# A state-space convolution, two adapter layers and a gated FFN on one core: group 3's tables earlier, later chunks' results through DRAM, 29 weights ahead

## The chip, the core and the metric

The kernel runs on one core of one Trainium2 chip. The metric is the device time of one execution, in microseconds. All data is float32. The engines named below are TensorE (PE, matmuls), VectorE (DVE), ScalarE (ACT), GpSimd (POOL) and SyncE (SP), which only issues transfers. All transfers of the core run on the same 16 DMA engines.

## The reference

Four residual layers on x of shape (32, 64, 1024), that is batch B, channels H, positions L:

```python
x = x + ssm(x, log_dt, C, log_A_real, A_imag, D, length)     # y*mask, y = irfft(rfft(u)*rfft(K)) + u*D
x = x + einsum('bsi,boi->bso', x, w1[adapter_ids])           # 1024 x 1024 of 16, one per batch row
x = x + einsum('bij,bkj->bik', x, w2[adapter_ids2])
x = x + down(silu(gate(x)) * up(x))                          # 1024 -> 2752 -> 1024, each with a rank-16 LoRA
```

K is the convolution filter of a channel, `2*Re(sum_n Ct[n]*exp(dtA[n]*l))` for l below 1024. The first layer is thus a causal convolution along the 1024 positions, separately for 64 channels; `mask` cuts it off at each row's length. The second and third need one 4 MB matrix for each batch row and layer, the fourth the same three matrices for all rows.

## The kernel before

Rows are worked in four chunks of eight batch rows (512 columns); a chunk is a tile `x` of 128 positions x 8 x 512. TensorE executes in program order; on the other engines a scheduler places the instructions, with `issue_after` as a lower bound where it is written.

**Setup and convolution** (`convolution`, from line 600). SyncE loads the parameters (`par`), constants, lengths and then x of all four chunks (L624; chunks 2 and 3 lie in a pool on the right side of SBUF). VectorE, ScalarE and GpSimd make the filters of the 64 channels in nine groups of 4, 4, 8, ... 8 channels (`kernels(g)`): GpSimd multiplies out `rho` and `br` (L698), VectorE reduces angles (L645), ScalarE takes exponentials and sines, VectorE forms `et` and `gt` (the last at L791). TensorE then multiplies `gt` and `et` into a PSUM tile `pk` (L804), after a matmul (L795) that puts the D of each channel into it: its moving operand `dk` is a mostly zero tile of 32 columns a channel, filled by GpSimd. ScalarE copies `pk` to `ks` and stores it to DRAM as `kp`, one tensor a group, each with 128 zeros ahead (L815, L816).

`convolve` takes four channels at a time: it loads the reversed x of these channels (`uf`), then for each pair of channels the filter's shifted rows from DRAM (`hk`, L833, three buffers), does 32 matmuls (L845), and VectorE applies the mask (`tmp`). At the end GpSimd adds `tmp` to the x of each of the four chunks (L861). Groups 0 and 1 are made ahead; group g+2 is made after the first four channels of group g. So TensorE's stream reads: tables 0 and 1, channels 0 to 3, table 2, channels 4 to 7, table 3, channels 8 to 11, table 4, and so on.

**Adapters** (`adapter`, L163). One adapter is eight weight tiles of 512 KB (`wa`, rows taken by the batch row's index, L179) and 64 matmuls (L184). VectorE transposes the result and adds it to x (L195, L197). The 16 adapters of chunk 0 run by themselves. Their first nine weights go to tiles `early`, loaded where SyncE has room after the sixth filter load; all later weights of the kernel, those of the FFN too, share a pool `wpool` of nine tiles of 512 KB. A weight's tile is given again once its last reader is done.

**FFN** (`ffn`, L458). `rest` (L401) multiplies the odd columns left over. `gated` (L346) then runs ten times, with two steps each (gate, up). A step loads two weight tiles (`wf`), VectorE forms sums of them (`stationary`), and TensorE does seven products of four matmuls (L361) where eight would be plain (Strassen-like); VectorE collects them in `c` (L378 to L390). After each step `between` is called: at step 0 of chunk 0 it parks x of chunks 2 and 3 in DRAM and gives their place to the activations' pool `apool`; at step 0 of chunks 1 and 2 it loads the next x from there; and at each step it runs `other(4)`, which spreads the 16 adapters of the next chunk over the 20 steps (4 shares each) and five of the eight down-projection parts (5 shares each): 16 adapters in 105 shares. The down projection (L558) follows in two blocks, with the outputs of the chunk stored at the end.

Of the kernel before, what the change touches and what calls it, by code (L numbers as in the profile page):

```python
# [8 lines left out]
F32 = mybir.dt.float32  # L9
I32 = mybir.dt.int32  # L10
AF = mybir.ActivationFunctionType
ALU = mybir.AluOpType
# [4 lines left out]
P = 128  # L17
B, H, L = 32, 64, 1024
NS = 64
KT = L // P  # L20
# [9 lines left out]
EARLY = 9  # L30
# [6 lines left out]
NPIECE = 2 * BC  # L37
AT_GATED, AT_DOWN = 4, 5
# [27 lines left out]
def kernel(  # L66
# [44 lines left out]
    def x_tile(pool, c, tag):  # L111
        return pool.tile([P, KT, TC], F32, tag=tag, name=f"x{c}")

    ctx.enter_context(tc.manual_schedule(engines={PE}))
    xs = [x_tile(xpool, c, "x") for c in range(2)]

    right = ExitStack()
    x2pool = right.enter_context(tc.tile_pool(name="x2pool", bufs=1, side="right"))
    first = right.enter_context(ExitStack())
    epool = first.enter_context(tc.tile_pool(name="epool", bufs=1, side="right"))  # L120
    late = [x_tile(x2pool, c, f"x{c}") for c in range(2, NCK)]
    early = [epool.tile([P, L], F32, tag=f"e{i}", name=f"early{i}") for i in range(EARLY)]
    blocks = convolution(tc, cst, consts, xt, xf, ssm, lens, xs + late, ps_tile)
    parked = []

    def park():
        for c, x_c in enumerate(late, 2):
            d = dpool.tile([P, KT, TC], F32, tag=f"xd{c}", name=f"xd{c}")
            nc.gpsimd.dma_start(d, x_c)
            parked.append(d)  # L130

    ids_sb = cpool.tile([1, 3 * B], I32, tag="ids", name="ids_sb")
    nc.sync.dma_start(ids_sb, ids)

# [25 lines left out]
    loads = []  # L160
    ypool = ctx.enter_context(tc.tile_pool(name="ypool", bufs=2, reuse_waits="tile"))

    def adapter(w, layer, b):  # L163
        c, lo = b // BC, (b % BC) * H
        with ExitStack() as after:
            if len(loads) > 3:

                after.enter_context(tc.issue_after(loads[-4]))
            e = nc.values_load(
                ids_sb[0:1, layer * B + b : layer * B + b + 1],  # L170
                engines=[SP],
                min_val=0,
                max_val=NE - 1,
            )
        acc = ps_tile(f"pa{layer}_{b}")
        for kt in range(KT):
            name = f"wa{layer}_{b}_{kt}"
            wt = early.pop(0) if early else wpool.tile([P, L], F32, tag="w", name=name)
            load = nc.sync.dma_start(  # L179
                wt, w[bass.ds(e, 1), kt].rearrange("e p f -> p (e f)")  # L180
            )
# [11 lines left out]
        loads.append(load.ins)  # L193
# [5 lines left out]
    def adapters(c):  # L199


        for b in range(c * BC, (c + 1) * BC + 1):
            if b < (c + 1) * BC:
                yield adapter(w1, 0, b)
            if b > c * BC:
                yield adapter(w2, 1, b - 1)

    with tc.issue_after(blocks[5]):

        pieces = adapters(0)  # L210
        for _ in range(3):
            next(pieces)
    for _ in pieces:
        pass
# [18 lines left out]
    apools = []  # L233
# [112 lines left out]
    def gated(c, m, xb, between):  # L346
# [4 lines left out]
        for g, w in enumerate((wg, wu)):  # L351
# [38 lines left out]
            nc.vector.tensor_add(cf, cf, lt[:, g].rearrange("p i t -> p (i t)"))  # L390
# [3 lines left out]
        act = apools[0].tile([P, 2, TC], F32, tag="act", name=f"act_{c}_{m}")  # L394
# [63 lines left out]
    def ffn(c, xb, others):  # L458
# [6 lines left out]
        def other(share, of=2 * FM * AT_GATED + (2 * KH - 3) * AT_DOWN):  # L465
            due[0] += share * NPIECE
            while due[1] * of < due[0]:
                next(others, None)
                due[1] += 1

        def between(i):
            if i == 0 and c == 0:
                with tc.issue_after(cols[-1]):
                    park()
                right.close()
                apools.append(
                    ctx.enter_context(
                        tc.tile_pool(
                            name="apool", bufs=MB, side="right", reuse_waits="tile"
                        )  # L480
                    )
                )
            if i == 0 and c and c + 1 < NCK:
                x_n = x_tile(xpool, c + 1, "x")
                nc.sync.dma_start(x_n, parked[c - 1])
                xs.append(x_n)
            other(AT_GATED)
# [3 lines left out]
        for block, (m0, m1) in enumerate(BLOCKS):  # L491
# [7 lines left out]
            if last:  # L499
# [3 lines left out]
                for t in (0, 1):  # L503
                    wl_t = wl[:, t].rearrange("p i f -> p (i f)")
                    gather(wl_t[FIRST], bd, rows_half[FIRST, c, t : t + 1])
                    nc.sync.dma_start(wl_t[SECOND], wd_rest)
# [5 lines left out]
            for i, act in enumerate(acts):  # L512
                t3 = apools[0].tile([P, 4, TH], F32, tag="actd", name=f"actd_{c}_{m0 + i}")
# [86 lines left out]
def convolution(tc, cst, consts, xt, xf, ssm, lens, xs, ps_tile):  # L600
# [9 lines left out]
    with ExitStack() as ctx:  # L610
# [12 lines left out]
        for c in range(NCK):  # L623
            nc.sync.dma_start(xs[c], xt[:, c])  # L624
# [141 lines left out]
        zero = s1.tile([HG, P], F32, tag="zero", name="zero")  # L766
        nc.vector.memset(zero, 0.0)


        dk = s1.tile([P, HG, LQ], F32, tag="dk", name="dk")  # L770
        nc.gpsimd.memset(dk, 0.0)

        def kernels(g):
# [3 lines left out]
            r = powers(g, y, s1, "r")  # L777
            nc.gpsimd.tensor_copy(dk[0:1, :n, 0], dskip[0:1, h0 : h0 + n])
# [15 lines left out]
            ps = ps_tile(f"pk{g}")[:LQ, : n * LQ]  # L794
            nc.tensor.matmul(  # L795
                ps,
                cst[:, CO_SEL : CO_SEL + LQ],
                dk[:, :n].rearrange("p h l -> p (h l)"),
                start=True,
                stop=False,  # L800
                skip_group_check=True,
            )
            for i in range(n):
                nc.tensor.matmul(  # L804
                    ps[:, i * LQ : (i + 1) * LQ],
                    gt[:, i, :],
                    et[:, i, :],
# [227 lines left out]
```

## Time and profile before

| | us |
|---|---|
| median of three runs (2400.56 to 2403.77) | 2400.56 |
| the profiled execution, whole | 2400.47 |
| its span, first to last instruction | 2398.8 |
| TensorE busy | 2324.7 (97%) |
| VectorE busy | 1087.4 (45%) |
| ScalarE busy | 310.8 (13%) |
| GpSimd busy | 206.8 (9%) |

A profile shows one execution. The span is cut into 40 slices of about 60 us; a digit is the busy share of an engine in tenths, and GB/s is what the DMA engines moved:

```profile
PE   4998888999999999999999999999999999999999
DVE  7511113454344543554344533554444544554653
DMA  7889997656656646656756646655756543223311
GB/s 274 286 290 369 408 408 273 217 211 210 228 202 226 226 149 213 228 202 211 244 189 244 208 148 215 242 189 201 269 182 248 185 158 115 82 84 108 99 55 62
```

The first slice is the setup, up to the third or fourth is the convolution, the next three are chunk 0's adapters, and all the rest are the four FFNs. A group of the profile names line, engine, operation, `out<-in` by tile names (buffer numbers left out), and what the engine waited for before it.

### The profile page before, as it was taken

The page shows a single profiled execution, that of the slowest core. Times are in us where ns is not written, and L with a number is a line of the kernel's source. Part 1 is how long each engine was busy: PE and PEld are TensorE (multiplying, and loading weights), DVE is VectorE, ACT ScalarE, POOL GpSimd, SP SyncE. Part 2 cuts the span into 40 slices and gives each one's busy share as a digit, 9 for nine tenths or more (in the row PEclk, how much of TensorE's full clock was granted, in tenths as well). Part 3 has the DMA queues.
Part 4 walks back from the last instruction along what each step waited for, and adds up shares of the span by engine and source line. Part 5 has one row for each costly group of instructions (what it writes and reads, how often), then busy time and mean ns, then how long its engine had stood idle before and what let it go on. Part 6 is the DMA issues. An engine that isn't in the chain of part 4 may idle for free.

```text
span 2398.8 us, 46172 instructions
## 1 busy us (share of the span) xinstructions
PE 2324.7 (97%) x19154; PEld 1837.2 (77%) x19154; DVE 1087.4 (45%) x2067; ACT 310.8 (13%) x605; POOL 206.8 (9%) x301
## 2 busy tenths in 40 slices
PE   4998888999999999999999999999999999999999
PEld 3995335787787786788787786788787787888888
DVE  7511113454344543554344533554444544554653
ACT  4200002110011101110011101110011101210210
POOL 3533001000000020000000020000000020000000
PEclk9999999999999999999999999999999999999999
DMA  7889997656656646656756646655756543223311
GB/s 274 286 290 369 408 408 273 217 211 210 228 202 226 226 149 213 228 202 211 244 189 244 208 148 215 242 189 201 269 182 248 185 158 115 82 84 108 99 55 62
DMA packets 163139, 501.21 MB, mean 209 GB/s; under 512 B 20018, under 2 KB 54130, under 8 KB 161906
## 3 DMA queue, kind: packets, MB, share of 16 engines
q1 hardware_dynamic: 146434, 461.78, 55.2%
q0 software_dynamic: 9568, 27.80, 3.6%
q10 hardware_dynamic: 6928, 8.69, 1.0%
q8 instruction: 151, 2.47, 0.4%
q14 instruction: 58, 0.48, 0.1%
HBM read 485.31 MB, written 12.88 MB: 208 GB/s over the span
## 4 chain that ended last, share of the span: by engine, by line
PE 90%; DMA 7%; DVE 1%; ACT 1%; issue 0%; POOL 0%; SPq 0%; ACTq 0%; DVEq 0%; POOLq 0%
PE pf L361 41%; PE po L558 20%; PE pa L184 15%; DMA wa<-in_w 6%; PE pc L845 5%; PE pr L421 3%; PE po L553 2%; PE pe L305 2%; PE pl_d L277 1%; PE pl_u L277 0%; PE pl_g L277 0%; DVE br L645 0%; DMA ln<-in_lens 0%; DMA hk<-kp 0%; DMA kp<-ks 0%
## 5 line engine op out<-in xcount | busy, mean ns | idle before, releaser
L361 PE MATMUL pf<-xd,wf 128*128 128x256 f32 x2560 | 607.2, 381 | 0.0
L361 PEld LDWEIGHTS pf<-xd,wf 128*128 128x128 f32 x2560 | 481.6, 190 | 75.4 <-issue 7.4
L184 PE MATMUL pa<-wa,x 128*32 128x256 f32 x8048 | 468.8, 382 | 28.0 <-DMA wa<-in_w 26.4
L361 PE MATMUL pf<-xd,s 128*128 128x256 f32 x1920 | 453.7, 379 | 2.3 <-ACT c L377 2.3
L184 PEld LDWEIGHTS pa<-wa,x 128*32 128x32 f32 x8048 | 248.2, 110 | 241.2 <-DMA wa<-in_w 70.5
L361 PEld LDWEIGHTS pf<-xd,s 128*128 128x128 f32 x1920 | 364.7, 190 | 52.3 <-ACT c L377 2.7
L845 PE MATMUL pc<-uf,hk 128*128 128x256 f32 (+7 forms) x1024 | 151.8, 311 | 11.8 <-DMA hk<-kp 11.8
L221 POOL DMA_INDIRECT bgu<-in_bgu,rows x44 | 45.5, 1033 | 1354.8 <-PE pe L305 1305.7
L558 PE MATMUL po<-act,wd 128*128 128x256 f32 x640 | 161.7, 383 | 0.0
L845 PEld LDWEIGHTS pc<-uf,hk 128*128 128x128 f32 x1024 | 147.3, 194 | 15.9 <-issue 12.0
L558 PE MATMUL po<-actd,wd 128*128 128x256 f32 x640 | 159.0, 379 | 0.0
L558 PE MATMUL po<-actd,s 128*128 128x256 f32 x640 | 159.0, 379 | 0.0
L386 DVE TENSOR_TENSOR c<-pf,u 128x256 f32<-128x256 f32 x80 | 34.0, 425 | 242.3 <-PE pf L361 242.3
L558 PEld LDWEIGHTS po<-act,wd 128*128 128x128 f32 x640 | 119.4, 190 | 22.9 <-issue 6.3
L558 PEld LDWEIGHTS po<-actd,wd 128*128 128x128 f32 x640 | 121.6, 190 | 16.5
L558 PEld LDWEIGHTS po<-actd,s 128*128 128x128 f32 x640 | 121.6, 190 | 16.5
L315 ACT COPY lt<-pe 128x512 f32<-128x512 f32 x160 | 82.2, 599 | 307.5 <-PE pe L305 216.1
L195 DVE STREAM_TRANSPOSE y<-pa 128x512 f32<-128x512 f32 x64 | 45.5, 711 | 142.0 <-PE pa L184 142.0
L390 DVE TENSOR_TENSOR c<-c,lt 128x1024 f32<-128x1024 f32 x80 | 98.0, 1225 | 6.4
L333 DVE TENSOR_TENSOR s<-wf 128x512 f32<-128x512 f32 x80 | 54.7, 684 | 89.3 <-DMA wf<-in_wg 43.3
L333 DVE TENSOR_TENSOR s<-wd 128x384 f32<-128x384 f32 x64 | 31.2, 487 | 129.7 <-PE po L558 95.8
L421 PE MATMUL pr<-x,wr 128*128 128x512 f32 x192 | 84.2, 595 | 0.0
(166 smaller groups left out, 1816.6 us busy)
## 6 DMA issues: line engine op xcount, KB each, us to landing
wa<-in_w SPq DMA_DIRECT2D x503, 512.0 KB
wf<-in_wg SPq DMA_DIRECT2D x80, 512.0 KB
wf<-in_wu SPq DMA_DIRECT2D x80, 512.0 KB
wd<-in_wd SPq DMA_DIRECT2D x96, 384.0 KB
hk<-kp SPq DMA_DIRECT2D x30, 1024.0 KB
x<-in_xt SPq DMA_DIRECT2D x4, 2048.0 KB
uf<-in_xf SPq DMA_DIRECT2D x16, 512.0 KB
wd<-in_wd SPq DMA_DIRECT2D x32, 256.0 KB
```

What stands on the lines that cost most here:

```text
L184: nc.tensor.matmul(acc[i * S : (i + 1) * S, s * 256 : (s + 1) * 256], xs[c][:, kt, lo + s * S : lo + (s + 1) * S], wt[:, i * 256 : (i + 1) ...
L195: nc.vector.transpose(y, acc)
L221: nc.gpsimd.indirect_dma_start(out=t, out_offset=None, in_=table, in_offset=bass.IndirectOffsetOnAxis(ap=at_, axis=0),)
L305: nc.tensor.matmul(ps[:, at_ * 2 * H : (at_ + 1) * 2 * H], bt[pair(j), g], tms[table][pair(j)], start=(g == 0), stop=True, skip_group_chec ...
L315: nc.scalar.copy(lt[:, :n, 2 * H * j : 2 * H * (j + 1)], ps[:, : n * 2 * H].rearrange("p (i t) -> p i t", i=n),)
L333: nc.vector.tensor_add(s1, a21, a22)
L361: nc.tensor.matmul(ps, ws[j][:, kt, :], xb[j][:, kt, :], start=start and kt == 0, stop=kt == KH - 1, skip_group_check=True,)
L390: nc.vector.tensor_add(cf, cf, lt[:, g].rearrange("p i t -> p (i t)"))
L421: nc.tensor.matmul(ps, wt[:, kt, :], xs[c][:, kt, :], start=(kt == 0), stop=(kt == KT - 1),)
L553: nc.tensor.matmul(pss[j], w, a, start=False, stop=False, skip_group_check=True)
L558: nc.tensor.matmul(pss[j], ws[j][:, i, :], ab[m - m0][j], start=(m == m0 and home[j] % 2 == 0), stop=(m == m1 - 1), skip_group_check=True,)
L845: nc.tensor.matmul(ps[:, j, d * B :], hk[:, j, d * P : (d + 1) * P], uf[:, i + j, : KT - d, :].rearrange("p k b -> p (k b)"), start=(d == ...
```

## The change

- **Places for weights.** `early` has 16 tiles, and four more in the place of an x tile (`place`, later x of chunk 1). With the nine of `wpool` this makes 29. A generator `weights` issues the loads of all adapters in their order; `fetch`, called in each `convolve` after the load of `uf`, takes eight from it at the first four channels and one at each later one. `adapter` uses what has come and asks for the rest. `ids_sb` is now loaded first of all.
- **Later chunks.** Only x of chunk 0 is loaded at the start. GpSimd adds `tmp` to it, copies the results of the other three chunks to `co` and stores them to DRAM (`cd`, 1 KB for each partition and chunk). In the FFN of chunk c, `bring` loads x of chunk c+1 and its results, a quarter of the channels in each `wpool` tile, at steps 0 and 2; `take` has VectorE add them at steps 2 and 4, after the last addition to `c` of that step. The five steps 0 to 4 run no adapters; the 16 adapters spread over 85 shares. Parking falls away, and `apool` is there from the start of the FFN.
- **Tables.** `between` of `convolve` makes the next group between the two pairs of channels, if fewer than g+3 are made. So table 2 stands in TensorE's stream after two channels and not four, and each later one two channels earlier.
- **D.** `par` holds D in row 0 and zeros below. A matmul of the selector with these columns adds D to column 0 of each channel after the filter's products; `dk` falls away.
- **Filters in DRAM** are one tensor `kps`; its zeros are stored once by GpSimd.

The core of the diff (lines left out marked):

```diff
-EARLY = 9
+EARLY = 16
+FIRST_LOADS = 8
+PLACES = EARLY + 4 + 9
+HA = 4
+STEPS = 5
...
+    place = x_tile("_early")
+    xs = [x_tile(0)]
...
+    early += [
+        place[:, i : i + L // TC].rearrange("p k t -> p (k t)")
+        for i in range(0, KT, L // TC)
+    ]
+    cd = dpool.tile([NCK - 1, P, H // HA, HA * KT * BC], F32, tag="cd", name="cd")
...
+    def weights():
+        for layer, b in (at_ for c in range(NCK) for at_ in layers(c)):
...
+            for kt in range(KT):
+                name = f"wa{layer}_{b}_{kt}"
+                wt = early.pop(0) if early else wpool.tile([P, L], F32, tag="w", name=name)
+                w = (w1, w2)[layer]
+                load = nc.sync.dma_start(
+                    wt, w[bass.ds(e, 1), kt].rearrange("e p f -> p (e f)")
+                )
...
+                yield wt
...
+    def fetch(ha):
+        for _ in range(FIRST_LOADS if ha == 0 else 1):
+            if len(ahead) < PLACES:
+                ahead.append(next(stream))
...
+    def bring(c, quarters):
+        if quarters[0] == 0:
+            xs.append(x_tile(c))
+            with tc.issue_after(loads[2 * BC - 1]):
+                nc.sync.dma_start(xs[c], xt[:, c])
+        n = H // HA // 4
+        for q in quarters:
+            t = wpool.tile([P, n * HA, KT * BC], F32, tag="w", name=f"cv{c}_{q}")
+            with tc.issue_after(loads[2 * BC - 1]):
+                nc.sync.dma_start(
+                    t.rearrange("p i k -> p (i k)"),
+                    cd[c - 1, :, q * n : (q + 1) * n].rearrange("p g e -> p (g e)"),
+                )
+            came[q] = t
+
+    def take(c, quarters):
+        n = H // 4
+        for q in quarters:
+            xv = xs[c].rearrange("p k (b h) -> p (k b) h", h=H)[:, :, q * n : (q + 1) * n]
+            with tc.issue_after(last_add[-1]):
+                nc.vector.tensor_add(xv, xv, came.pop(q).rearrange("p i k -> p k i"))
...
-            wt = early.pop(0) if early else wpool.tile([P, L], F32, tag="w", name=name)
-            load = nc.sync.dma_start(
-                wt, w[bass.ds(e, 1), kt].rearrange("e p f -> p (e f)")
-            )
+            wt = ahead.pop(0) if ahead else next(stream)
...
-        def other(share, of=2 * FM * AT_GATED + (2 * KH - 3) * AT_DOWN):
+        def other(share, of=(2 * FM - STEPS) * AT_GATED + (2 * KH - 3) * AT_DOWN):
...
         def between(i):
-            if i == 0 and c == 0:
-                with tc.issue_after(cols[-1]):
-                    park()
...
-            if i == 0 and c and c + 1 < NCK:
-                x_n = x_tile(xpool, c + 1, "x")
-                nc.sync.dma_start(x_n, parked[c - 1])
-                xs.append(x_n)
-            other(AT_GATED)
+            if i < STEPS:
+                if c + 1 < NCK:
+                    if i in (2, 4):
+                        take(c + 1, (i - 2, i - 1))
+                    if i in (0, 2):
+                        bring(c + 1, (i, i + 1))
+            else:
+                other(AT_GATED)
...
-        for c in range(NCK):
-            nc.sync.dma_start(xs[c], xt[:, c])
+        nc.sync.dma_start(x0, xt[:, 0])
...
-            nc.tensor.matmul(
-                ps,
-                cst[:, CO_SEL : CO_SEL + LQ],
-                dk[:, :n].rearrange("p h l -> p (h l)"),
...
+            nc.tensor.matmul(
+                ps[:, :, 0],
+                cst[:, CO_SEL : CO_SEL + LQ],
+                dskip[:, h0 : h0 + n],
...
+            uf = s3.tile([P, HA, KT, B], F32, tag="uf", name=f"uf{ha}", bufs=2)
+            nc.sync.dma_start(uf, xf[:, ha : ha + HA])
+            fetch(ha)
...
+                if i:
+                    between()
                 ps = ps_tile(f"pc{ha + i}").rearrange("p (i t) -> p i t", i=2)
...
-            for c in range(NCK):
-                xv = xs[c].rearrange("p k (b h) -> p k b h", h=H)[:, :, :, ha : ha + 4]
-                nc.gpsimd.tensor_tensor(xv, xv, tv[:, :, c * BC : (c + 1) * BC, :], ALU.add)
+            xv = x0.rearrange("p k (b h) -> p k b h", h=H)[:, :, :, ha : ha + HA]
+            tv = tmp.rearrange("p i (k b) -> p k b i", b=B)[:, :, :BC, :]
+            nc.gpsimd.tensor_tensor(xv, xv, tv, ALU.add)
+            co = s1.tile([P, NCK - 1, HA * KT, BC], F32, tag="co", name=f"co{ha}")
+            tv = tmp.rearrange("p i (k c b) -> p c (i k) b", k=KT, b=BC)[:, 1:]
+            nc.gpsimd.tensor_copy(co, tv)
+            nc.gpsimd.dma_start(
+                cd.rearrange("c p g e -> p c g e")[:, :, ha // HA],
+                co.rearrange("p c i b -> p c (i b)"),
+            )
...
-                if i == 0 and g + 2 < len(GROUPS):
-                    ready.append(kernels(g + 2))
+            def more():
+                if len(ready) < min(g + 3, len(GROUPS)):
+                    ready.append(kernels(len(ready)))
+            for i in range(0, n, HA):
+                convolve(ready[g], i, h0 + i, more)
```

## The prediction, made before the changed kernel ran

> **What bounds the kernel now.** I read the span line and the engine times first, then the chain of waits, the TensorE timeline, the issue queue of SyncE, and windows of DMA share and rate. TensorE is busy for 2324.7 us, 97% of the span, so only places where it waits, or runs slowly because its data trickles in, are worth anything.
>
> ```profile
> 33.44 10.90 PE L845 MATMUL pc<-uf,hk 128*128 128x256 f32 x64 [8.44 <-DMA hk<-kp]
> ...
> 45.32 9.38 PE L845 MATMUL pc<-uf,hk 128*128 128x256 f32 x64
> 54.64 0.62 PE L795 MATMUL pk<-dk,cst 128*32 128x256 f32 x2
> 55.09 0.67 PE L804 MATMUL pk<-bet,bgt 128*32 128x32 f32 x16
> 59.13 11.01 PE L845 MATMUL pc<-uf,hk 128*128 128x256 f32 x64 [3.37 <-DMA hk<-kp]
> ...
> 149.40 46.19 PE L845 MATMUL pc<-uf,hk 128*128 128x256 f32 x320
> ...
> 359.80 0.40 PE L277 MATMUL pl_g<-x,at_g 128*32 128x128 f32 x6
> ...
> 406.19 7.11 PE L184 MATMUL pa<-wa,x 128*32 128x256 f32 x128
> ```
>
> Columns: start, us, engine, line, operation, count, idle before it and its releaser. Three stages stand out. Up to 33.44 TensorE waits for the first shifted filter rows (`hk`). From 33.44 to 195.5 is the convolution, 9.2 us for each four channels (46.1 for the last 20), with one stall of 3.37 us; 64 matmuls after either wait take 10.9 to 11.0 us and not 9.38. From 195.5 to 359.8 are chunk 0's 16 adapters. Later adapters take 7.11 us each, so these would need 113.8 us; they take 164.3. The chain of waits says why:
>
> ```profile
> 245.00 10.10 DMA wa<-in_w
> 255.21 10.10 DMA wa<-in_w
> ```
>
> Eight loads of 512 KB per 10.21 us: 1.277 us a load at 408 GB/s, which is saturation. After 390 the chain is TensorE nearly without gaps, with adapters of the next chunk between FFN products. So the end of the kernel moves with the end of chunk 0's adapters. The issue queues tell what may move:
>
> ```profile
> 2.30 11.52 SPq L624 DMA_DIRECT2D x<-in_xt  x4
> ...
> 29.32 1.75 SPq L833 DMA_DIRECT2D hk<-kp  x4
> ...
> 52.86 0.89 SPq L833 DMA_DIRECT2D hk<-kp  x2
> ```
>
> ```profile
> 22.04 0.34 ACTq L816 DMA_DIRECT2D kp<-ks  x1
> ...
> 51.27 0.31 ACTq L816 DMA_DIRECT2D kp<-ks  x1
> ```
>
> ```profile
> 150.00:187.00 37.00, 37.00 (x259) 36.18 (x258) 5.43 (x8) 0.00 (x0) 12.22 (x16) 1.00 0.85 292
> q0 software_dynamic: 752, 1.84, 10.7%
> ```
>
> The first two fences are the issue queues of SyncE and ScalarE (start, us, queue, line, transfer, count); in the third stand a window of the late convolution and the GpSimd queue's row from 187 to 240 us (packets, MB, share). The first filter store (`kp<-ks`) took 7.3 us to release its load, the third 1.6. Late in the convolution DMA is busy 0.85 of the time at 292 GB/s (the last two numbers of the window), so there is some, not much, room for weights. Only nine adapter weights are issued before the end of the convolution, five of them after the last filter (182.4 to 186.3 on SyncE's queue).
>
> **What the Trainium skill says.** "DMA: Bandwidth & Descriptors", Queues, rings and completion order: each DMA engine goes round its queue rows packet by packet. That agrees with a small store lagging 7.3 us under 8 MB of x loads and 1.6 us on a quiet system. Same page, Specifications: pieces of 512 B or more run at line rate; here GpSimd's 1.84 MB (adapter columns in 512 B pieces, gathered rows) took 10.7% of the 53 us from 187, or 324 GB/s, not quite 408. "TensorE: Matmul & The Clock Gate", Part 1: after an idle window the clock is halved until activity releases it; the 10.9 and 11.0 against 9.38 agree. "Advanced Engine Details and Errata", Memory Cachelines: an access pattern that touches a new 16-byte line each time is penalised. The new VectorE adds read at 256 B stride; no row of VectorE shows such a read.
>
> **Part by part** (against the profiled execution: span 2398.8, whole 2400.47, 1.67 around it; the median of three runs is 2400.56, so nothing has to be shifted).
>
> 1. *First filter earlier.* Ahead of the first store there were 8.4 MB of x and 0.5 MB of `uf`. Now: 2.1 MB of x, 0.5 MB of `uf`, 4.2 MB of weights. 6.8 MB at 408 GB/s is 16.7 us; from about 3 us it drains at 20, before the store at about 22.4 (`ids_sb` now stands first in SyncE's queue and delays `par` by some 0.4 us, the 0.46 us between two issues there). The store then needs 1.6 us, the loads go out at 24.2 and, with 4.1 us as before, TensorE starts at about 28.5. I take 28.7: -4.7 us (bounds 0, if the weights still clog the engines at 22 us, and -5.3). GpSimd's four register loads, now ahead of its table products, must fit before 8.5 us; they should.
>
> 2. *Third group between the first channels.* Its `bgt` ended at 34.73; VectorE now starts the group about 0.8 us sooner, because GpSimd makes `br` before `brho`. So the tables are ready at 33.9, and the first two channels end at 28.7+5.5 = 34.2: TensorE should not wait. The evacuation on ScalarE stands behind the sine of the fourth group (39.3), the store goes out near 40.4, the load near 42.3, and lands at about 48.5, while channel 8 is needed at 49.9. The 3.37 us stall goes, and with it the slow restart of 11.01-9.38 = 1.63: -5.0 (bound 0, if a new wait of that size stands at `pk`; the margins are 0.3 and 1.4 us). The next tables come every 10 us, channels in groups of 18.6: nothing is late after.
>
> 3. *D through a small matmul.* In each of seven groups the `dk` matmul held TensorE for 0.45 us (54.64 to 55.09); a moving operand of 8 columns should take 0.1: -2.4 (bounds -3, -1.5).
>
> Together the convolution would end at 195.5-12.1 = 183.4.
>
> 4. *More DMA in the convolution.* Per four channels: 2.62 MB of `hk` and `uf`, one weight (1.28 us), and 0.39 MB of results written in 1 KB pieces. With several in flight `hk` ran at 410 to 420 GB/s (57 to 64 us), so 6.3+1.28+1.2 (at 324) = 8.8 us against TensorE's 9.2: covered. With the rate per busy share in the window (292/0.85 = 344) it is 7.6+1.28+1.2 = 10.1, or 0.9 too long, 12 us over 13 rounds. Bounds 0 and +12; I take +3, since `hk` has three buffers but is issued only as TensorE frees one: 186.4. GpSimd does one add of 0.85 us, a copy and a DMA issue where it did four adds (3.3 us), so it stays inside 9.2.
>
> 5. *Adapters of chunk 0.* 23 weights are asked for in the convolution (8+15) and the six that fill 29 places behind the last filter. But only the nine of `wpool` are used again. Load 30 waits until TensorE has used weight 21: 21 x 0.889 = 18.7 us into the stage. In that time DMA stands nearly still, and GpSimd's 1.84 MB fit into it. Then 99 loads x 1.277 = 126.4 us, 2 us to the first landing, and 2 us for the last products and hiccups: 149.4 against 164.3, -14.9. TensorE's own 113.8 is not reached. The stage ends at 335.8 instead of 359.8: -24.0.
>
> 6. *FFN.* 6.3 MB of x and 6.3 MB of results are read in five steps without adapters; each step's 1 MB of weights leaves DMA idle most of 13 us, and the slots' addresses show that the copies take slots that later steps get back in time. Adapters go from 16 in 105 shares to 16 in 85; consecutive adapter steps already ran at 406 to 432 without a stall. VectorE gets 12 adds of 1024 elements. Contiguous ones take 1.23 us. Behind the first pair in its queue stands the `c` add that must free its bank before the sixth product of the next step, 8.7 us in; without the adds it is there at 5.7, with them at 8.2. Cost: 0 if as quick as 1.23; 1 to 2 us a chunk at double. I take +1.5 in all.
>
> Sum: -24.0+1.5 = -22.5; 2400.5-22.5 = 2378.
>
> **Rivals.** *DMA becomes the bound of the convolution* (part 4 at its upper end, +9 on the forecast): 2387. For it: 0.85 busy already. Against: that share is measured with one load in flight, and 420 GB/s were reached. *All covers hold* (no drag, no FFN cost, 3 us more from shorter landings): 2370. *It does not do what it says*: the prefetched weights arrive, but the stop for slots lasts longer or a new wait stands at the third group's tables, and of 24 us some 5 to 9 stay: 2394. Against: adapters' places are plain from the addresses. *Slower*: the strided VectorE adds. If each takes four times 1.23, 4.9 us, a pair needs 9.8 where 3.0 (step 2) and 4.5 (step 4) are free: 6.8+5.3 = 12.1 us in three chunks, 36 us: 2412. It decides from about 3.8 us an add, where the stalls eat the gain. For it: the skill's penalty. Against: L197 reads runs of 32 at the full rate (691 ns for 512), and half of this add's operands are contiguous.
>
> **Numbers.** Forecast 0.50, DMA-bound 0.22, all covers 0.14, does not do it 0.07, slower 0.07. The forecast's own range is 2373 to 2384. Holding 8 in 10 takes in the better case and most of the DMA-bound one: 2367 to 2392. Within 0.2% (2395.7 to 2405.3, which a measurement hardly tells from no change) falls part of the last two: faster 0.88, same 0.06, slower 0.06.
>
> **What would show it.** First `pc` at 28 to 29; no wait at channel 8; convolution rounds still 9.2 us (10 or more: DMA-bound); the last channel at 183 to 190; a DMA lull some 15 us into the adapters and then 10.2 us per eight loads to about 336; VectorE adds L204 near 1.3 us. The forecast is wrong if rounds stretch, if the first filter is still at 33, if TensorE waits at L836, or if products after L204 wait for VectorE.

## The result, and the profile after

| | before | changed |
|---|---|---|
| median of 20 runs each, us | 2402.17 (2400.56 to 2403.77) | 2398.76 (2393.99 to 2402.47) |
| profiled execution, span, us | 2398.8 | 2396.6 |
| end of the convolution | 195.51 | 193.13 |
| end of chunk 0's adapters | 359.80 | 349.51 |
| from there to the end | 2039.0 | 2047.1 |

The ratio is 0.9985, 95% interval 0.9978 to 0.9992: 0.15% faster, where 0.9% was forecast. The FFN of chunk 0 starts 10.3 us earlier, and 8.1 us of that are lost again after it. By stages of the profiled execution the forecast was missed by 6.7 us in the convolution (186.4 forecast), by 7.0 in the adapters (149.4 forecast, 156.4 measured) and by 6.6 in what follows (+1.5 forecast, +8.1 measured): together the 20.3 us between the -22.5 us that were forecast and the -2.2 us of the two spans.

The convolution first, in the TensorE timeline of the changed kernel (start, us, engine, line, operation, count, idle before and its releaser):

```profile
29.66 6.89 PE L886 MATMUL pc<-uf,hk 128*128 128x256 f32 x32 [4.31 <-DMA hk<-kp]
36.48 0.69 PE L836 MATMUL pk<-bet,bgt 128*32 128x32 f32 x16
37.01 0.21 PE L845 MATMUL pk<-par,cst 128*32 128x8 f32 x2
37.15 9.38 PE L886 MATMUL pc<-uf,hk 128*128 128x256 f32 x64
...
111.85 4.76 PE L886 MATMUL pc<-uf,hk 128*128 128x256 f32 x32 [1.50 <-DMA hk<-kp]
...
133.18 6.36 PE L886 MATMUL pc<-uf,hk 128*128 128x256 f32 x32 [1.99 <-issue]
...
193.13 0.64 PE L241 MATMUL pa<-early,x 128*32 128x256 f32 x8
```

The first filter is 3.8 us earlier (33.44 before), no wait is left at channel 8, and a table's block between channels takes 0.67 us (36.48 to 37.15) where it took 1.05. But from 90 us on there are six waits of 0.2 to 2.0 us, 5.5 in sum, and 32 matmuls after one of them take 6.36 us and not 4.76. Channel 12 begins at about 61.8 (57.11, where channel 10 begins, and 4.7 for two channels), where it began at 71.12 before: 9.3 us ahead. At the end of the convolution 2.4 us of that are left.

The pause of the transfers in the adapters is there (each line: window; its length, busy us of PE, weight loads (PEld), DVE, ACT, POOL, then TensorE's granted clock as a share of full speed, DMA share, GB/s):

```profile
190.00:200.00 10.00, 8.87 (x129) 6.32 (x131) 0.69 (x1) 0.00 (x0) 5.14 (x9) 1.00 0.59 224
200.00:210.00 10.00, 10.00 (x192) 6.00 (x188) 2.82 (x4) 1.05 (x1) 4.99 (x8) 1.00 0.22 66
210.00:220.00 10.00, 10.00 (x193) 6.01 (x188) 1.41 (x3) 0.00 (x0) 4.30 (x8) 1.00 0.79 238
220.00:230.00 10.00, 7.26 (x120) 3.20 (x116) 1.41 (x2) 0.00 (x0) 0.00 (x0) 1.00 1.03 367
```

SyncE issues nothing from the stage's start to 212.87. In the FFN of chunk 0 a new wait stands before the first gated step. TensorE's timeline, and GpSimd's:

```profile
371.29 7.13 PE L470 MATMUL pr<-x,wr 128*128 128x512 f32 x16
383.39 1.24 PE L353 MATMUL pe<-tm_g,bgu 32*128 32x128 f32 x16 [4.96 <-DMA bgu<-in_bgu,rows]
384.38 1.10 PE L353 MATMUL pe<-tm_u,bgu 32*128 32x128 f32 x16
385.41 3.77 PE L409 MATMUL pf<-xd,wf 128*128 128x256 f32 x8
```

```profile
373.76 0.54 POOL L297 DMA_DIRECT2D raw_d<-in_ad  x1 [0.64 <-issue]
374.94 0.54 POOL L297 DMA_DIRECT2D raw_d<-in_ad  x1 [0.64 <-issue]
378.35 1.19 POOL L267 DMA_INDIRECT bgu<-in_bgu,rows  x1 [2.87 <-issue]
```

The tile `bgu` has been free since 371.3, when its last reader was done, yet the gather goes out at 378.35: eight loads of the second block's columns (`raw_d`, from 368.41) stand ahead of it in GpSimd's queue. In the kernel before, the parking (`xd<-x`) and one of these eight loads went ahead of the gather, seven came behind it, and TensorE waited 1.50 us for it. GpSimd's timeline of the kernel before, and TensorE's, with a second wait that the changed kernel no longer has:

```profile
372.60 1.07 POOL L129 DMA_DIRECT2D xd<-x  x2 [0.66 <-DMA raw_d<-in_ad]
377.05 0.55 POOL L249 DMA_DIRECT2D raw_d<-in_ad  x1 [3.38 <-ACT at_d L254]
382.04 1.00 POOL L221 DMA_INDIRECT bgu<-in_bgu,rows  x1 [4.44 <-PE pe_rest L305]
```

```profile
390.22 0.73 PE L305 MATMUL pe<-tm_g,bgu 32*128 32x128 f32 x16 [1.50 <-DMA bgu<-in_bgu,rows]
...
399.09 1.99 PE L361 MATMUL pf<-xd,s 128*128 128x256 f32 x8 [2.32 <-ACT c L377]
```

VectorE's twelve adds take 1.96 us each, as the group shows (duration min/median/max in ns); TensorE has four short stalls behind them (0.92, 0.94, 0.60 and 1.40 us), of which the longest stands below:

```profile
L204 DVE TENSOR_TENSOR x<-x,cv x12: 1922/1958/1983, 428.0 to 1530.1; 128x1024 f32<-128x1024 f32 x12
```

```profile
1509.41 1.99 PE L409 MATMUL pf<-xd,s 128*128 128x256 f32 x8 [1.40 <-DVE c L430]
```

### The profile page after: what moved, and what is told of

The parts are those of the page before. It is cut to its first block, busy times and chain, and to the rows that moved or that the text cites. A ratio compares the mean times of both kernels' runs of the same rounds, so it can differ in the third digit from the quotient of the medians.

```text
span 2396.6 us, 46124 instructions
## 1 busy us (share of the span) xinstructions
PE 2321.4 (97%) x19154; PEld 1838.7 (77%) x19154; DVE 1098.6 (46%) x2078; ACT 309.7 (13%) x605; POOL 190.2 (8%) x275
## 5 line engine op out<-in xcount | busy, mean ns | idle before, releaser
L241 PE MATMUL pa<-wa,x 128*32 128x256 f32 x7872 | 454.9, 381 | 24.5 <-DMA wa<-in_w 21.9
L241 PEld LDWEIGHTS pa<-wa,x 128*32 128x32 f32 x7872 | 241.9, 110 | 230.1 <-DMA wa<-in_w 60.8
```

What stands on the lines that cost most here:

```text
L241: nc.tensor.matmul(acc[i * S : (i + 1) * S, s * 256 : (s + 1) * 256], xs[c][:, kt, lo + s * S : lo + (s + 1) * S], wt[:, i * 256 : (i + 1) ...
```

## The experiments

Each run is compared with the kernel before on the same chip. The kernel before had medians of 2400.98 to 2402.20 in these comparisons, so a difference between the medians of two rows can be off by a microsecond from that alone. "Stage" is the time from the end of the convolution to the first `pl_g`, which is the first product of the FFN. The comments after `#` in the code below are added.

| run | median, us | ratio to before, 95% | end of convolution | stage |
|---|---|---|---|---|
| changed kernel | 2398.76 | 0.9985 (0.9978, 0.9992) | 193.1 | 156.4 |
| e1 gather first | 2392.45 | 0.9962 (0.9949, 0.9976) | 193.9 | 156.4 |
| e2 nine places first | 2395.23 | 0.9965 (0.9951, 0.9979) | 198.2 | 151.4 |
| e3 no later weights | 2393.03 | 0.9967 (0.9954, 0.9980) | 185.5 | 160.1 |
| e4 no results stored | 2390.87 | 0.9953 (0.9938, 0.9969) | 187.6 | 155.7 |
| e5 adds in runs of 4 | 2393.98 | 0.9962 (0.9949, 0.9976) | 193.2 | 156.7 |
| e6 tables back | 2399.58 | 0.9990 (0.9984, 0.9997) | 192.2 | 155.9 |
| e7 places again | 2384.80 | 0.9930 (0.9917, 0.9944) | 193.2 | 143.9 |
| e8 same row, even | 2400.68 | 0.9998 (0.9989, 1.0006) | 196.8 | 155.4 |
| e9 same row, odd | 2400.21 | 0.9993 (0.9984, 1.0001) | 195.9 | 155.3 |
| b2 = e1 + e5 + e7 | 2375.70 | 0.9896 (0.9881, 0.9911) | 191.5 | 144.7 |
| b3 = b2 + e3 | 2381.95 | 0.9917 (0.9903, 0.9931) | 184.6 | 160.9 |
| b4 = b2 + fourth hk | 2376.83 | 0.9894 (0.9878, 0.9911) | 194.1 | 146.8 |
| c1 = b2 + longer lead | 2372.38 | 0.9877 (0.9861, 0.9894) | 186.0 | 149.0 |
| c2 = b2 + weight behind | 2370.34 | 0.9869 (0.9853, 0.9886) | 187.7 | 144.9 |

In the runs that keep the changed kernel's loads of the convolution and their order, the convolution ends anywhere from 191.5 (b2) to 198.2 (e2), so a difference of 2 or 3 us there, in one profile, says little.

**The wait for bgu (e1).**

```diff
+    gathers[c, piece] = got.ins            # in b_rows
...
+                if behind is not None:     # in columns, for each load
+                    after.enter_context(tc.issue_after(behind))
...
-            at = columns(ad[:, block, :, :n], c, n, f"d{block}_{c}")
+            at = columns(ad[:, block, :, :n], c, n, f"d{block}_{c}", gathers.get((c, 0)))
```

> Against the changed kernel (its profile: TensorE waits 4.96 us at 383.39 for the rows bgu, then restarts slowly, about 2.8 us more), only the order of GpSimd's queue is altered: the second block's eight column loads (raw_d) come behind the first bgu gather of the chunk. Theory (GpSimd's queue is what holds bgu, the rows' place being free from 371.3): the gather is issued at about 371.5 to 373, lands before 378.4, the wait and the slow restart go, 5 to 8 us less in all: 2391 to 2394 us. Rival (the wait only passes to another releaser, such as the activation copy that cost the kernel before 2.32 us at 399, or the second gather then comes late): at most 2 us less, 2397 to 2399.

Only the order on GpSimd is changed. GpSimd's and TensorE's timelines of e1:

```profile
361.86 0.54 POOL L302 DMA_DIRECT2D raw_d<-in_ad  x1 [0.63 <-DMA raw_d<-in_ad]
372.51 1.00 POOL L269 DMA_INDIRECT bgu<-in_bgu,rows  x1 [10.11 <-PE pe_rest L358]
373.82 0.56 POOL L302 DMA_DIRECT2D raw_d<-in_ad  x1 [0.31 <-ACT lt_rest L368]
```

```profile
372.06 7.13 PE L475 MATMUL pr<-x,wr 128*128 128x512 f32 x16
379.12 0.73 PE L358 MATMUL pe<-tm_g,bgu 32*128 32x128 f32 x16
379.67 0.62 PE L358 MATMUL pe<-tm_u,bgu 32*128 32x128 f32 x16
380.22 1.99 PE L414 MATMUL pf<-xd,wf 128*128 128x256 f32 x8
```

The gather goes out as soon as its tile is free and the products follow without a gap, at full clock: the granted clock is 1.00 from 379.1 to 382.0, where it was 0.50 from 383.4 to 389.0 in the changed kernel. From the first `pr` of chunk 0 to that of chunk 1 it takes 536.8 us and not 544.4: 7.7 us, the 4.96 of the wait and 2.7 of the slow restart. The two waits that the kernel before had here (1.50, and 2.32 for ScalarE at 399) have not come back, so nothing took its place.

**The places (e2, e7).** e2 puts the nine `wpool` places first; e7 also gives the sixteen `epool` places again, for three turns.

```diff
-    wt = early.pop(0) if early else wpool.tile([P, L], F32, tag="w", name=name)
+    if early and taken[0] >= 9:                          # e2
+        wt = early.pop(0)
+    else:
+        wt = wpool.tile([P, L], F32, tag="w", name=name)
...
+    if EARLY + 9 <= n < PLACES:                          # e7, n-th weight
+        return spare[n - EARLY - 9]
+    n = n if n < PLACES else n - 4
+    if n < 3 * (EARLY + 9) and n % (EARLY + 9) >= 9:
+        return epool.tile([P, L], F32, tag="e", name=name, bufs=EARLY)
+    return wpool.tile([P, L], F32, tag="w", name=name)
```

> Against the changed kernel, the first nine adapter weights lie in the pool of nine tiles that are given again, and the twenty tiles used once come after, so load 30 waits for weight 1 and not for weight 21. Theory (the DMA lull at 193 to 213 us is made by the order of places; without it the rest of the stage is bound by DMA): 99 loads at 1.277 us, about 5 us each for GpSimd's columns and for the FFN's first tiles, 2 us to the first landing: stage end near 332 in place of 349.5, 17 us less, 2380 to 2384 us; if GpSimd's transfers and the FFN's first tiles find room elsewhere, up to 25 us less. Rival (the lull cost nothing, since TensorE lived on the 29 weights and DMA moved other things then): less than 4 us less, above 2394. Second rival: the gain at the stage's end is lost again in chunk 0's FFN, where bgu comes late anyway: stage end 17 us earlier, time less than 8 us less.

> Against the changed kernel, sixteen of the twenty places used once are given again for three turns, together with the nine of the pool, and the nine come first; so each load of the first 79 waits only for a weight some 25 back. Theory (DMA's pause in the adapters is set by the places, and putting the nine first only moved it from 197..213 to 218..230 us because nine slots still were all that came free): no pause, DMA at 400 GB/s or so from the stage's start, 99 loads at 1.277 us and about 8 us for GpSimd's columns and the FFN's first tiles: stage 138 to 144 us in place of 156.4, time 12 to 18 us less: 2381 to 2387. Rival (GpSimd's columns must now wait for these places and come at the stage's end): stage as short, but the first low-rank products wait, gain under 8 us.

Windows of e2, then of e7:

```profile
210.00:220.00 10.00, 9.99 (x185) 7.04 (x181) 1.41 (x2) 1.05 (x1) 4.71 (x7) 1.00 1.02 346
220.00:230.00 10.00, 10.00 (x193) 8.36 (x187) 2.82 (x4) 0.00 (x0) 2.54 (x4) 1.00 0.41 112
```

```profile
200.00:210.00 10.00, 10.00 (x192) 6.05 (x188) 2.72 (x4) 0.00 (x0) 3.18 (x5) 1.00 1.02 392
210.00:220.00 10.00, 10.00 (x192) 6.02 (x188) 1.50 (x3) 0.00 (x0) 0.00 (x0) 1.00 1.03 406
220.00:230.00 10.00, 10.00 (x195) 5.99 (x186) 2.04 (x3) 0.00 (x0) 0.00 (x0) 1.00 1.03 406
```

e2's expectation was wrong by its own counting. The first nine places come free early and take 9 x 1.277 = 11.5 us of loads, but the tenth load takes a place that holds weight 30 by then, and waits until that is used: 30 x 0.889 = 26.7 us in, and not 18.7. (SyncE issues it at 226.16, 27.9 us after the stage's start; in the changed kernel the first load after the pause goes out 19.7 us after it.) That is worth an estimated 11.5 - 8.0 = 3.5 us. The median is 3.5 us lower; the stage is 5.0 shorter in the profiled execution, where the convolution happened to end 5.1 later, so the stage's end did not move. By its time alone e2 would fit the rival, that the pause cost nothing (less than 4 us less); e7 decides against that. In e7, where a place comes back from 25 weights ago, the rate stays at 392 GB/s or more and the stage is 12.5 us shorter, the time 14.0. Its edit changes nothing but the places, so the pause is shown to cost 12 to 14 us.

**The adds (e5).**

```diff
-    co = s1.tile([P, NCK - 1, HA * KT, BC], F32, tag="co", name=f"co{ha}")
-    tv = tmp.rearrange("p i (k c b) -> p c (i k) b", k=KT, b=BC)[:, 1:]
-    nc.gpsimd.tensor_copy(co, tv)
+    co = s1.tile([P, NCK - 1, KT, BC, HA], F32, tag="co", name=f"co{ha}")
+    tv = tmp.rearrange("p i (k c b) -> p c k b i", k=KT, b=BC)
+    for c in range(1, NCK):
+        nc.gpsimd.tensor_copy(co[:, c - 1], tv[:, c])
```

The store, the loads in `bring` and the add in `take` use the same order.

> Against the changed kernel, GpSimd writes the results to co with the four channels innermost (three copies for one), so that VectorE's twelve adds (L204, 1.96 us each with reads 256 B apart) read runs of four elements. Theory (the adds' reads make them slow, and they make the stalls of 0.92, 0.94, 0.60 and 1.40 us behind the c additions): adds near 1.23 us, those stalls gone, about 4 us less: 2393 to 2396. Rival 1 (runs of 16 B cost as much as single elements): adds still 1.9 us, stalls as before, time within 1.5 us. Rival 2 (adds quicker but the stalls stay, since the five steps without adapters leave the c addition no cover anyway): less than 1.5 us less. GpSimd's three copies should take some 2.5 us of a round of 9.2 and more, and cost nothing.

The group of e5:

```profile
L205 DVE TENSOR_TENSOR x<-x,cv x12: 1216/1218/1221, 428.3 to 1525.1; 128x1024 f32<-128x1024 f32 x12
```

The adds cost no more than contiguous ones, no stall is left behind them, and chunks 0 to 2 take 1.1, 1.2 and 2.3 us less: 4.6 together, and the median is 4.8 lower.

**What stretches the convolution (e3, e4, e8, e9).**

```diff
-        for _ in range(FIRST_LOADS if ha == 0 else 1):   # e3
+        for _ in range(FIRST_LOADS if ha == 0 else 0):
...
+    with tc.issue_after(last_hk):                        # e3, after convolution
+        while len(ahead) < PLACES:
+            ahead.append(next(stream))
...
-            nc.gpsimd.dma_start(                             # e4
-                cd.rearrange("c p g e -> p c g e")[:, :, ha // HA],
-                co.rearrange("p c i b -> p c (i b)"),
-            )
...
-                    cd[c - 1, :, q * n : (q + 1) * n].rearrange("p g e -> p (g e)"),
+                    xt[:, c, 2 * q : 2 * q + 2].rearrange("p k t -> p (k t)"),
...
-                            offset=kp[row + i + j : row + i + j + 1, 1:2].offset,
-                            ap=[[1, P], [KROW, n], [1, L]],
+                            offset=kp[row + i + j : row + i + j + 1, P : P + 1].offset,   # e8; e9 keeps 1:2
+                            ap=[[0, P], [KROW, n], [1, L]],                               # e8, e9
```

> Against the changed kernel, the convolution brings only the eight first weights; the other 21 are asked for after its last filter load. Theory A (the drag in the convolution is the sum of all bytes on the DMA engines): without 15 x 0.52 MB, some 19 us of transfers, the waits for hk go and the convolution ends at 185 to 187 in place of 193.1; what left it must be moved later, so the adapters end near 350 to 354 and the time stays within 5 us of the changed kernel's: 2396 to 2404. Theory B (the drag comes from the results' stores in 1 KB pieces, not from weights): the convolution still ends at 191 or later, and the stage ends 10 to 15 us later: 2409 to 2414.

> Left out of the computation: the convolution's results of chunks 1 to 3 are formed in co but not stored, and the FFN adds a part of x of the same size in their place, so the outputs of these chunks differ. Theory A (sum of bytes): 6.3 MB less in 16 rounds, 0.39 MB or about 1.1 us a round; the waits for hk mostly go, the convolution ends at 185 to 188 in place of 193.1, and the time falls by 4 to 8 us. Theory B (the weights are the drag): the convolution ends at 191 or later, time within 2 us. If both this run and the one without later weights end the convolution near 185, the two share one limit.

> Left out of the computation: the shift of the filter from one partition to the next. All 128 partitions of hk read the same 4 KB, which begins at a multiple of 512 B; the values are wrong, all instructions and bytes as in the changed kernel. Theory (the filter rows, each beginning 4 B after the last one, are what holds the convolution's transfers at 353 GB/s at a share of 0.95, where the weights alone move 408 at 1.03): waits for hk gone, convolution end 184 to 187 in place of 193.1. Rival (start addresses do not matter; it is the number of bytes, or the stores): convolution end within 2 us of 193.

> Left out of the computation: as in the run with all partitions on one row, but the row begins 4 B after a multiple of 512 B. If the odd start is what costs: convolution end near 193 as in the changed kernel, while the even one is shorter. If it is the overlap of rows (many transfers reading the same addresses): both runs differ from the changed kernel by the same amount. If neither matters: both within 2 us of 193.

Without the fifteen later weights no wait is left after the first filter, and without the stores about three quarters of the drag goes (193.1 to 187.6, of 7.6): TensorE's timeline of e3, and the windows of e3 and of the changed kernel:

```profile
134.64 50.93 PE L890 MATMUL pc<-uf,hk 128*128 128x256 f32 x352
185.50 0.64 PE L244 MATMUL pa<-early,x 128*32 128x256 f32 x8
```

```profile
50.00:175.00 125.00, 125.00 (x933) 121.89 (x932) 45.20 (x81) 20.96 (x34) 43.41 (x51) 1.00 0.93 320
```

```profile
50.00:175.00 125.00, 119.38 (x875) 115.78 (x874) 42.44 (x74) 21.16 (x34) 39.24 (x49) 0.99 0.95 353
```

So either addition alone is nearly covered and the two together are not; theory A of either run gave these ends rightly, but that the limit is the sum of bytes is refuted below (c1). The fifteen weights brought there did harm: the kernel without them is 4 to 6 us faster (0.9967 against 0.9985, with intervals that just overlap; medians 5.7 apart), below the expected 2396 to 2404. That the pause ate what they should have saved fits b3 below, where without a pause they do save time. Where the filter rows begin made no difference that shows: e8 and e9 end within 0.9 us of each other, and neither is earlier than the changed kernel. Both are later than the 2 us about 193 that the rival gave, if inside the spread named above; whether 128 partitions that read one address cost something, the third case of e9's expectation, stays open.

**The tables (e6).**

```diff
-                convolve(ready[g], i, h0 + i, more)
+                convolve(ready[g], i, h0 + i, lambda: None)
+                if i == 0:
+                    more()
```

> Against the changed kernel, the tables of group g+2 stand again after four channels and not after two. Theory (part 2 of the prediction: the order took away 3.37 us of waiting and 1.63 of slow restart): a wait of 2 to 4 us at channel 8, convolution end at 196 to 198 in place of 193.1, 3 to 5 us more: 2401 to 2404. Rival (from 90 us on the convolution runs at the rate of its transfers, so time lost ahead of that is found again, because the transfers run on while TensorE waits): the wait at channel 8 is there, but the waits of 0.3 to 2 us later shrink by as much, convolution end 192 to 195, time within 1.5 us.

TensorE's timeline of e6:

```profile
53.43 11.01 PE L886 MATMUL pc<-uf,hk 128*128 128x256 f32 x64 [1.65 <-DMA hk<-kp]
65.03 18.59 PE L886 MATMUL pc<-uf,hk 128*128 128x256 f32 x128
...
192.19 0.64 PE L241 MATMUL pa<-early,x 128*32 128x256 f32 x8
```

The wait at channel 8 and the slow 64 matmuls after it are back (1.65 and 11.01), channel 12 begins 3.2 us later than in the changed kernel (65.03 against 61.8), and the convolution ends no later; the medians differ by 0.8 us, where 3 to 5 were expected, and the intervals of the two ratios overlap. The rival held: at most a small part of what was gained ahead of the late loads was kept.

**The three edits together, and without the later weights (b2, b3).**

> The three edits together: first bgu gather ahead of the second block's columns, results with the four channels innermost, places given again. If the gains are in different places and add: 7 and 4 and 15 us less than the changed kernel, 2370 to 2376. If one hides another (a stall of the FFN that stands in for the next): 2377 to 2384.

> Against the three edits together: no weight is brought in the convolution after the first eight; the other 21 are asked for behind its last filter load. Without the places given again, leaving these weights out of the convolution made the kernel 5.7 us faster, because they only lengthened the convolution by 7.6 us and DMA then paused. Theory (once DMA does not pause, a weight brought in the convolution saves its 1.277 us later): convolution end 184 to 186, but 15 loads more to do, 19 us, in the adapters: time 9 to 13 us more than with them, 2385 to 2389. Rival (bytes cost the same wherever they are moved): within 3 us of 2375.7.

The gains nearly add: 6.3 + 4.8 + 14.0 = 25.1 us singly, 23.1 together, by the medians. In b3 the convolution ends 6.9 us earlier and the stage is 16.2 longer, so once there is no pause the weights are worth 9.4 us at the stage's end (8.6 by the two profiled spans; 6.2 by the medians). That lies between the expected 9 to 13 and the rival's 3.

**Rate or lead (b4, c1, c2).** Is 353 GB/s all that the transfers carry of this mixture, or do the loads go out too late?

```diff
-            uf = s3.tile([P, HA, KT, B], F32, tag="uf", name=f"uf{ha}", bufs=2)
+            uf = s3.tile([P, HA, KT, B], F32, tag="uf", name=f"uf{ha}", bufs=3)     # c1
...
-                hk = s3.tile([P, 2, L], F32, tag="hk", name=f"hk{ha + i}")
+                hk = s3.tile([P, 2, L], F32, tag="hk", name=f"hk{ha + i}", bufs=4)  # b4 and c1
...
                 if i:
+                    if ha:                                                          # c2
+                        with tc.issue_after(got.ins):
+                            fetch(ha)
                     between()
```

> Against the three edits together: hk has four buffers in place of three, paid for with two of the sixteen places. Theory (the convolution's waits come from single loads that land late: a load goes out when its buffer is free, some 9.4 us before it is needed, and takes 8.5 us in the middle, so that uf, a weight or a store ahead of it makes it late, while over a round of 9.3 us 3.5 MB would need only 376 GB/s): with one more pair of channels in hand the waits of 0.3 to 1.6 us mostly go, convolution end at 184 to 187 in place of 191.5, time 3 to 7 us less: 2369 to 2373. Rival (the transfers cannot carry more than some 355 GB/s of this mixture): the first waits come later but the convolution ends at 190 or later, time within 2 us of 2375.7.

> Against the three edits together: three buffers of uf in place of two and four of hk in place of three, paid for with three of the sixteen places. Each pair of filters can now go out when the pair before the last has been used, and uf no longer stands in the way. Theory (late loads: lead, not rate): waits in the convolution gone but for the first rounds, its end at 184 to 187 in place of 191.5, time 3 to 7 us less: 2369 to 2373. Rival (the transfers carry no more than some 355 GB/s of this mixture): waits only start later, end at 189 or later, time within 2 us of 2375.7 or longer, since three places fewer are there.

> Against the three edits together: in each later round the weight's load stands in SyncE's queue behind the round's filter loads and not ahead of them. Theory (order: 0.5 MB ahead of the filters makes them 1.3 us late): waits of 0.3 to 1.6 us mostly gone, convolution end at 185 to 188 in place of 191.5, time 3 to 6 us less. Rival (rate): the same 0.5 MB then stands ahead of the next uf and the next filters, end at 190 or later, time within 2 us of 2375.7.

A fourth filter buffer alone did nothing (194.1, 2376.83 us), which is what b4's rival, the rate, had forecast. SyncE's queue shows another reason: it is worked in order, the next `uf` has to wait for one of two tiles, and the filters stand behind it. From 85 to 185 us SyncE waited 39.6 us for `uf` tiles and 36.9 us for filter buffers in the changed kernel; in b4 it waited 72.3 us for `uf` tiles and no longer for filter buffers. The queue of the changed kernel, then of c2:

```profile
110.38 0.35 SPq L865 DMA_DIRECT2D uf<-in_xf  x1
111.53 0.36 SPq L161 DMA_DIRECT2D x_early<-in_w  x1
111.94 5.08 SPq L873 DMA_DIRECT2D hk<-kp  x2
122.02 0.35 SPq L865 DMA_DIRECT2D uf<-in_xf  x1
```

```profile
100.30 0.35 SPq L882 DMA_DIRECT2D uf<-in_xf  x1
100.71 4.57 SPq L891 DMA_DIRECT2D hk<-kp  x2
105.47 0.35 SPq L172 DMA_DIRECT2D wa<-in_w  x1
```

In c1, with a third `uf` tile too, the filters get their lead, and in the window from 50 to 175 us the same mixture runs at 386 GB/s:

```profile
50.00:175.00 125.00, 123.99 (x925) 120.90 (x924) 44.05 (x75) 21.02 (x34) 54.21 (x78) 1.00 1.00 386
```

Its convolution ends at 186.0, with one wait of 1.01 us after the first filter; c2, which only puts 0.5 MB of weight behind the filters of its round, ends at 187.7. So the transfers do carry this mixture, and it was the lead and the order of the loads that made them late. The medians are 3.3 and 5.4 us below b2's; with four executions each the intervals of the ratios still overlap, so the ends of the convolution and its waits after the first filter (6.1 us in b2, 2.4 in c2, 1.0 in c1) carry the argument more than the times do. A third `uf` tile without the fourth filter buffer was not run. c2 is the fastest version run: 2370.34 us, 1.3% under the kernel before (0.9869, 0.9853 to 0.9886).

## Why the prediction was wrong, by its steps

1. *First filter earlier:* right in kind; the first filter came at 29.66, 28.7 was said.
2. *Third group between the first channels:* the wait and the slow restart went as said, but of the 5.0 us at most a small part reached the end of the convolution (e6).
3. *D:* 0.38 us a group, about what was taken (2.4 for seven).
4. *More DMA in the convolution* is the first term that failed. It allowed 3 us for weights and stores together, on top of 183.4. With the stores and without the fifteen later weights the convolution ends at 185.5 (e3), and these weights add 7.6 us, to 193.1: 9.7 us in all, inside the step's bounds of 0 to 12 but not near its 3. The working compared bytes with rates (8.8 to 10.1 us against 9.2) and did see that a filter load goes out only as a buffer comes free; it took that as a reason for a small term. It is the mechanism: a filter load goes out about one round ahead and takes 8.5 us to land (median of 50 to 175), so with one more load ahead of it in the queue it comes late, though the mean rate would do. The rival *DMA becomes the bound* named the place but not this cause, and c1 refutes the rate: with more lead the same traffic ends at 186.0, where the step had 186.4.
5. *Adapters of chunk 0* is the second. The pause was foreseen and is 19.7 us (193.13 to 212.87; 18.7 said), and in the steady part the loads follow each other by 1.28 us as said. What was sized at 2 + 2 us is about 10 (156.4 less 19.7 and 126.4; the step's own terms add up to 149.1, not to its 149.4). From 213 to 233 SyncE's queue moved 6.2 MB, where 8.2 fit (4.8 us). That this is because places come free one by one, so that few loads are out at first, is an inference. In the last 10 us the FFN's first tiles travel beside the last weights: 53.7 MB landed from 213 to 350 on that queue, 102.5 tiles for 99 (4.5 us). Both figures are from the queue's bytes; no run took away either alone. And the step priced the pause without asking whether it was needed: e7 removes it, for 12.5 us of the stage.
6. *FFN* is the third: +1.5 said, +8.1 measured. The text looked at the added VectorE work and at the queue of VectorE, not at what stands ahead of the `bgu` gather on GpSimd once the parking is gone: 7.7 us (e1). That the missing parking let the eight loads pass is read from the two timelines; e1 tests their order only. This was partly made up by the two stalls of the kernel before (1.50 and 2.32) that are gone. The adds take 1.96 us and cost 4.6 us (e5): 7.7 + 4.6 - 3.8 = 8.5, close to the 8.1. For adds at double 1.23 us the step itself said 1 to 2 us a chunk, which is what they cost; but it took 1.5 for all three chunks, leaning towards the contiguous case. "The Trainium skill", "Advanced Engine Details and Errata", Memory Cachelines, describes the cause: SBUF lines of 16 bytes, full rate while accesses stay in a line. The runs agree: reads 256 B apart took 1.6 times as long, runs of 16 B no longer than contiguous adds. The prediction cited the page for a rival at four times the price, not for the forecast's own sum.

## What to carry to other kernels

A prefetch into places that are used once saves as many loads as there are places and then stops the queue (19.7 us here): write down for each load which place it takes and when that comes back. Where each load goes out only as the work one round earlier ends, look at the issuing queue line by line: here order and lead decided (c1, c2) before the mean rate did, and time won ahead of that stage was not kept (e6). When a step is removed from an engine, read that engine's queue afterwards, for what now stands ahead of the next urgent instruction.

## What was not expected of the hardware

- A DMA share of 0.93 need not mean that little room is left: e3 moved 320 GB/s at 0.93 without a wait after the first filter, c1 386 at 1.00, the adapters of the changed kernel 408 at 1.03 (233 to 350 us).
- The start of the filter rows made no difference that shows: all partitions at one multiple of 512 B 342 GB/s (e8), all 4 B behind it 351 (e9), each 4 B behind the last one 353 (changed kernel). None of these ran at the limit of the transfers, as c1's 386 shows.
- VectorE's add of 1024 float32 with one operand read 256 B apart takes 1958 ns, in runs of 16 B 1218 (e5).
- Whether TensorE restarts slowly after a short wait does not follow from the wait's length alone: 32 matmuls of the convolution took 6.2 to 6.4 us after 1.99 (changed kernel), 2.79 (e2) and 3.87 us (b4), but the usual 4.76 after 2.21 (e1), 2.28 (e5) and 2.90 us (e8).
- A wait of 4.96 us of TensorE cost another 2.7 us through the slower clock after it (granted clock 0.50; `pe` 1.24 and 1.10 us for 0.73 and 0.62, the first `pf` 3.77 for 1.99). "The Trainium skill", "TensorE: Matmul & The Clock Gate", Part 1, describes such a restart, and the trace agrees.
